# Loading a resident adjacency matrix with converting transfers in place of staged loads and casts

## The chip, the cores and the metric

The kernel runs on one core of one Trainium2 chip. The metric is the device time of a run in microseconds (us). The runs of one kernel in one round of measurements lie within 0.1 to 0.5% of each other.

Engine names in the profile: PE is TensorE (matmul), PEld its weight loads, DVE is VectorE, ACT is ScalarE, POOL is GpSimd, SP is SyncE. L214 is line 214 of the kernel that a view belongs to.

## The reference, cut to what matters

Four graph layers in sequence on x (8 x 2048 x 64), each followed by a residual sum and a layer norm. All four use the same adjacency matrix, 2048 x 2048 of zeros and ones.

```python
x = layernorm(x + hypergraph(x, H, adj, ...))        # layer 0: softmax over H, degrees and product with adj
x = layernorm(x + gcn(x, adj, W))                    # layer 1
x = layernorm(x + chebyshev(x, emb, adj, ...))       # layer 2
x = layernorm(x + causal(x, adj, v, W1, b1, W2, b2)) # layer 3: three steps of adj @ v, relu, linear

# in layer 0:
h   = x @ W
deg = maximum(adj.sum(-1), 1.0)
industry = einsum('nm,bmf->bnf', adj / deg[:, None], x @ W_ind)
```

The matrix, 16.8 MB, is kept in SBUF all along, as 16 tiles of 128x2048 in float32r, the type in which this kernel gives it to TensorE.

## The kernel before: the parts that matter

**Loading.** Each tile comes in four pieces of 256 KB over SP's queue into one of four staging buffers; GpSimd casts each piece into the resident tile. Nine tiles are asked for early, two when the features are done with, five later.

```python
def staged(name):
    return hy.tile([P, JT, P], F32, tag="x", name=name, bufs=4)

def load_adj(t):
    for c in range(NCH):                       # NCH = 4
        a = staged("a").rearrange("p t f -> p (t f)")
        nc.sync.dma_start(a, adj_t[t * P:(t + 1) * P, cols(c)])
        tc.keep_in_program_order(nc.gpsimd.tensor_copy(adj[t][:, cols(c)], a))
```

**Part A of layer 0.** A set-up (masks, iotas, ranks, small loads on GpSimd's queue), then a loop over 16 tiles of nodes. Its first instructions on VectorE stand behind a copy of a small loaded vector, `av_col`:

```python
for dst, v in ((fcb_col, fc_b), (av_col, av)):
    nc.gpsimd.dma_start(dst, v.rearrange("(n o) -> n o", o=1))
...
nc.gpsimd.memset(avz, 0.0)
nc.vector.tensor_copy(avz[:, b, s], av_col.to_broadcast([P, F]))
...
for t in range(NT):                            # NT = 16
    ...  # ph: 4 matmuls of xt[t]
    nc.vector.tensor_scalar(sv, hv[...], CLIP, -CLIP, op0=ALU.min, op1=ALU.max)   # "seen"
    ...  # exps on ACT, st and ex on DVE
    nc.scalar.dma_start(hs_hbm[t * P:(t + 1) * P, :], st)
    nc.tensor.matmul(pagg[...], lhsT=m_n[:, t, :], rhs=ex[...])                   # twice
```

**The slot stage of layer 0.** First the one-hot matrices and the scores. Then 57 slots: for each a product `pz`, nine filler matmuls (column sums of the adjacency for the degrees first, then the product with x), a multiply of `pz` on VectorE, an exponential on ScalarE and so on.

**The check in the last layer.** Each piece of the matrix is loaded once more and compared with the resident tile; differences are counted.

```python
def check():
    t, k = checks.pop(0)                       # 64 of them
    a = fcav.rearrange("p i b f -> p (i b f)")
    nc.sync.dma_start(a, adj_t[t * P:(t + 1) * P, cols(k)])
    nc.vector.scalar_tensor_tensor(
        a, a, 1.0, adj[t][:, cols(k)].bitcast(F32), op0=ALU.mult, op1=ALU.not_equal,
        accum_out=left[:, t, k:k + 1],
    )
```

## Time and profile before

| what | before |
|---|---|
| median of 4 runs | 2236.3 us (2230.7 to 2238.3) |
| span of the profiled run | 2233.4 us |
| part A ends (last `pagg` matmul) | 72.5 us |
| first slot multiply on VectorE | 93.7 us |
| first product of layer 2 with the adjacency | 952.3 us |
| first check | 1703.1 us |

The busy line of the page gives, for each engine, busy us, share of the span and instructions. The DMA-issue line gives the destination and source, the engine, the count, the KB of each and the median us from issue to landing.

```profile
PE 1989.5 (89%) x7330; PEld 1284.9 (58%) x7330; DVE 1136.6 (51%) x1875; ACT 337.4 (15%) x620; POOL 563.5 (25%) x539
```

```profile
a<-in_adj_t SPq DMA_DIRECT2D x64, 256.0 KB, 4.3
```

They show that TensorE is busy over most of the span and that GpSimd, whose casts the change removes, is busy for a quarter of it. So the change can only pay in a stage in which something waits for a cast or for a staged load.

### The profile page before, as it was taken

To read this page: it belongs to the slowest core of one execution; us is meant where nothing else is said; L and a number is where in the kernel's file an instruction comes from. 1 tells how busy PE (TensorE), PEld (TensorE's weight loads), DVE (VectorE), ACT (ScalarE), POOL (GpSimd) and SP (SyncE) were. 2 spreads that over 40 slices of the span, in tenths; PEclk is the share of its full clock that TensorE was granted. 3 is DMA by queue.
4 is the path that set the end of the run, shared out by engine and by line. 5 is a ranking of instruction groups with operands and counts; after the bars stand their busy time and mean duration, and the time that the engine had idled before them with its cause. 6 is when DMAs were issued, how large, how long until landed. Compare 5 with 4: busy or idle time off the path is not lost.

```text
span 2233.4 us, 19857 instructions
## 1 busy us (share of the span) xinstructions
PE 1989.5 (89%) x7330; PEld 1284.9 (58%) x7330; DVE 1136.6 (51%) x1875; ACT 337.4 (15%) x620; POOL 563.5 (25%) x539
## 2 busy tenths in 40 slices
PE   6789978988858999899999999999986989999994
PEld 4567744655644444375456456447433767787873
DVE  6559956666533223215864772782784344331312
ACT  1133333223111111010010001001000011111110
POOL 4666657564323323200010110110010001020202
PEclk9889989999979999999999999999997999999997
DMA  8622233222210000000000000000001223200000
GB/s 279 213 81 96 86 105 105 80 72 66 76 45 0 19 19 19 10 33 5 7 7 3 7 10 0 10 7 3 7 7 28 76 71 82 70 20 1 19 1 21
DMA packets 72619, 104.31 MB, mean 47 GB/s; under 512 B 28080, under 2 KB 28128, under 8 KB 72320
## 3 DMA queue, kind: packets, MB, share of 16 engines
q1 hardware_dynamic: 63648, 87.29, 12.5%
q0 software_dynamic: 3552, 9.10, 1.6%
q10 hardware_dynamic: 5312, 6.56, 0.9%
q8 instruction: 60, 0.98, 0.2%
q14 instruction: 47, 0.39, 0.1%
HBM read 76.11 MB, written 26.80 MB: 46 GB/s over the span
## 4 chain that ended last, share of the span: by engine, by line
PE 57%; DVE 15%; DMA 12%; POOL 8%; issue 5%; ACT 2%; SPq 1%; ACTq 0%; POOLq 0%; DVEq 0%
PE py L1009 18%; PE u L177 12%; PE u L956 10%; PE u L565 9%; DMA fcav<-in_adj_t 7%; POOL ln_r L156 3%; DMA a<-in_adj_t 2%; PE ug L177 2%; DVE fcav L1103 2%; POOL gn L751 1%; PE pr L177 1%; DVE ln_c L146 1%; DVE ln_v L152 1%; DVE ln_m L144 1%; PE pf L177 1%
## 5 line engine op out<-in xcount | busy, mean ns | idle before, releaser
L1009 PE MATMUL py<-wp,xg 128*128 128x512 f32 x1024 | 448.6, 597 | 8.4 <-DVE fcav L1014 5.8
L1009 PEld LDWEIGHTS py<-wp,xg 128*128 128x128 f32 x1024 | 193.8, 191 | 254.2 <-issue 216.0
L177 PE MATMUL u<-adj,hi 128*128 128x512 f32 x768 | 256.7, 416 | 0.0
L177 PE MATMUL u<-adj,lo 128*128 128x512 f32 x768 | 246.7, 400 | 0.9 <-DVE lo L1068 0.9
L956 PE MATMUL u<-pt,xn 128*128 128x512 f32 x512 | 230.6, 610 | 8.3 <-DVE u L965 7.1
L1014 DVE TENSOR_TENSOR fcav<-py,emb_n 128x512 f32<-128x512 f32 x256 | 177.1, 692 | 52.0 <-PE py L1009 37.1
L1017 POOL TENSOR_TENSOR r<-r,bias 128x256 f32<-128x256 f32 x32 | 23.3, 729 | 636.1 <-DVE r L1015 636.1
L1015 DVE TENSOR_REDUCE r<-fcav 128x32 f32<-128x512 f32 x256 | 175.4, 685 | 8.1
L956 PEld LDWEIGHTS u<-pt,xn 128*128 128x128 f32 x512 | 98.7, 195 | 131.8 <-issue 116.9
L565 PE MATMUL u<-adj,vh 128*128 128x512 f32 x512 | 159.0, 410 | 14.6 <-ACT vh L168 10.8
L177 PEld LDWEIGHTS u<-adj,hi 128*128 128x128 f32 x768 | 143.3, 190 | 40.8 <-issue 11.6
L177 PEld LDWEIGHTS u<-adj,lo 128*128 128x128 f32 x768 | 144.8, 190 | 35.0 <-DVE lo L1068 1.3
L565 PE MATMUL u<-adj,vl 128*128 128x512 f32 x512 | 152.5, 399 | 0.0
L156 POOL TENSOR_TENSOR ln_r<-ln_e,neg_half 128x8 f32<-128x8 f32 x64 | 106.7, 1666 | 171.8 <-DVE ln_e L154 171.2
L950 DVE TENSOR_SCALAR pt<-pt 128x512 f32<-128x512 f32 x64 | 48.8, 780 | 176.6 <-ACT pt L949 175.1
L1087 POOL TENSOR_TENSOR r<-r,xn 128x512 f32<-128x512 f32 x16 | 20.4, 1277 | 419.5 <-DVE r L1086 419.5
L565 PEld LDWEIGHTS u<-adj,vh 128*128 128x128 f32 x512 | 96.5, 190 | 44.8 <-ACT vh L168 12.3
L954 POOL TENSOR_TENSOR acc<-acc,pt 128x512 f32<-128x512 f32 x60 | 79.6, 1327 | 165.7 <-DVE pt L950 162.9
L565 PEld LDWEIGHTS u<-adj,vl 128*128 128x128 f32 x512 | 96.9, 190 | 22.2 <-issue 0.7
L1103 DVE SCALAR_TENSOR_TENSOR fcav<-fcav,adj 128x512 f32<-128x512 f32 x64 | 44.8, 699 | 119.3 <-DMA fcav<-in_adj_t 119.1
L150 ACT ACTIVATE r<-ln_c 128x512 f32<-128x512 f32 x64 | 40.4, 631 | 283.8 <-DVE ln_c L146 274.0
L751 POOL DMA_INDIRECT gn<-gs_hbm,rank x64 | 69.5, 1086 | 38.8 <-PE pg L180 15.8
(331 smaller groups left out, 2765.4 us busy)
## 6 DMA issues: line engine op xcount, KB each, us to landing
a<-in_adj_t SPq DMA_DIRECT2D x64, 256.0 KB, 4.3
fcav<-in_adj_t SPq DMA_DIRECT2D x64, 256.0 KB, 2.9
x_hbm<-r SPq DMA_DIRECT2D x20, 256.0 KB, 2.1
hs_hbm<-st ACTq DMA_DIRECT2D x16, 292.0 KB, 4.7
xt<-in_x_t SPq DMA_DIRECT2D x16, 256.0 KB, 5.0
xc<-in_x_n SPq DMA_DIRECT2D x16, 256.0 KB, 2.8
gs_hbm<-acc SPq DMA_DIRECT2D x16, 256.0 KB, 2.0
u_hbm<-ut SPq DMA_DIRECT2D x16, 256.0 KB, 2.5
```

Source lines behind the costliest of these rows:

```text
L150: nc.scalar.activation(r, xc, AF.Square)
L156: nc.gpsimd.tensor_tensor(rstd, vare, neg_half[:, :groups], ALU.pow)
L177: tc.keep_in_program_order(nc.tensor.matmul(*args, **kw))
L565: nc.tensor.matmul(u[c], lhsT=half[:, j, :], rhs=adj[t][:, cols(c)], start=t == 0 and i == 0, stop=ends and not own,)
L751: nc.gpsimd.indirect_dma_start(out=gn[:, j, :], out_offset=None, in_=g_rows, in_offset=bass.IndirectOffsetOnAxis(ap=rank4[:, p, c * JT + j ...
L950: nc.vector.tensor_scalar(pt, pt, 1.0, None, op0=ALU.max)
L954: nc.gpsimd.tensor_tensor(acc, acc, pt, ALU.add)
L956: nc.tensor.matmul(u[p], lhsT=xn[p][:, t, :], rhs=pt, start=t == 0, stop=t == NT - 1)
L1009: nc.tensor.matmul(py.rearrange("p o d -> p (o d)"), lhsT=xg[b][:, q, cols(j, P)], rhs=wp[:, q, cols(k)], start=q == 0, stop=q == 1,)
L1014: nc.vector.tensor_tensor(pr, py, e_b, ALU.mult)
L1015: nc.vector.tensor_reduce(r[:, j, b, cols(k, OH)], pr, AX.X, ALU.add)
L1103: nc.vector.scalar_tensor_tensor(a, a, 1.0, adj[t][:, cols(k)].bitcast(F32), op0=ALU.mult, op1=ALU.not_equal, accum_out=left[:, t, k:k + 1],)
```

## The change

Its intent: no staging buffers, no casts, one DMA instruction for each 1 MB tile. The loads go to GpSimd's queue, since only it issues transfers that convert (the Trainium skill, "DMA: Bandwidth & Descriptors", section "SWDGE vs HWDGE vs iDMA"). Room for 14 early tiles (before: 12) comes from holding x's tiles in a ring of eight. The loads are paced by copies of one column on GpSimd, `seen_x`, which wait for x's tiles. The check of the last layer now compares the reloaded piece with its own float32r copy.

```diff
     def load_adj(t):
-        for c in range(NCH):
-            a = staged("a").rearrange("p t f -> p (t f)")
-            nc.sync.dma_start(a, adj_t[t * P:(t + 1) * P, cols(c)])
-            tc.keep_in_program_order(nc.gpsimd.tensor_copy(adj[t][:, cols(c)], a))
+        tc.keep_in_program_order(nc.gpsimd.dma_start(adj[t], adj_t[t * P:(t + 1) * P, :]))
...
-    XT = NT // 4
-    EARLY = 9
+    XT = NT // 8
+    XB = XT * NP
...
-        xt = [xs.tile([P, NP, P], F32, name=f"xt{t}") for t in range(NT)]
-        for t in range(NT):
-            nc.sync.dma_start(xt[t], x_t[t])
+        # fetch_xt(t): tile of a ring of XB = 8; eight ahead, then one for each turn of part A
...
-        for t in range(EARLY):
+        for t in range(NT - XT):
+            ahead = min(t + 4, XB - 1)
+            tc.keep_in_program_order(nc.gpsimd.tensor_copy(seen_x, xt[ahead][:, 0, 0:1]))
             load_adj(t)
...
-        for t in range(EARLY, EARLY + 2):
+        for t in range(NT - XT, NT):
             load_adj(t)
...
-        for t in range(EARLY + 2, NT):
-            load_adj(t)
...
-                fill(4 if t == 0 and s < 6 else 9)
+                fill(9)
...
             nc.sync.dma_start(a, adj_t[t * P:(t + 1) * P, cols(k)])
+            ar = lp.tile([P, C], F32R, tag="r", name="ar", bufs=1)
+            nc.scalar.copy(ar, a)
             nc.vector.scalar_tensor_tensor(
-                a, a, 1.0, adj[t][:, cols(k)].bitcast(F32), op0=ALU.mult, op1=ALU.not_equal,
+                a, a, 1.0, ar.bitcast(F32), op0=ALU.mult, op1=ALU.not_equal,
```

More of the change, by code (lines that the diff above doesn't have):

```diff
@@ L270, in tile_gnn_fast @@
         xs = xs_scope.enter_context(tc.tile_pool(name="xs", bufs=1, side="right"))
+        seen_x = pa.tile([P, 1], F32, name="seen_x")
         m_n = pa.tile([P, NT, E], F32, name="m_n")
@@ L275, in tile_gnn_fast, with fetch_xt @@
             nc.scalar.dma_start(m_en[c], h_en[:, cols(c)])
-        xt = [xs.tile([P, NP, P], F32, name=f"xt{t}") for t in range(NT)]
-        for t in range(NT):
-            nc.sync.dma_start(xt[t], x_t[t])
+        xt = {}
+        def fetch_xt(t):
+            if t < NT:
+                xt[t] = xs.tile([P, NP, P], F32, tag="xt", name="xt", bufs=XB)
+                nc.sync.dma_start(xt[t], x_t[t])
+        for t in range(XB):
+            fetch_xt(t)
         bd66 = pa.tile([P, 2, F + 2], F32, name="bd66")
@@ L425, in tile_gnn_fast @@
                 )
+            fetch_xt(t + XB)
             hv = ph[:, :, 0:G * (F + 2)].rearrange("p k (g c) -> p k g c", c=F + 2)
```

## The prediction

> **What bounds the kernel now.** I read the page's busy shares first: PE is at 89%, so over most of the span TensorE sets the time. The change touches only the load phase and the adjacency checks near the end, so I cut the span into windows of 25 us, the first six shown. The columns are window, its length, then busy us of PE, PE weight loads, DVE, ACT and POOL with counts, granted clock, DMA share, GB/s.
>
> ```profile
> 0.00:25.00 25.00, 7.71 (x58) 6.49 (x58) 13.67 (x52) 2.88 (x10) 9.65 (x43) 0.96 0.88 261
> 25.00:50.00 25.00, 20.47 (x106) 13.17 (x106) 16.48 (x51) 4.07 (x21) 10.99 (x20) 0.90 0.89 297
> 50.00:75.00 25.00, 18.56 (x88) 11.87 (x89) 15.24 (x43) 3.97 (x19) 9.22 (x16) 0.93 0.81 272
> 75.00:100.00 25.00, 20.69 (x92) 15.55 (x91) 11.23 (x27) 5.24 (x14) 21.08 (x35) 0.82 0.53 165
> 100.00:125.00 25.00, 17.17 (x44) 10.82 (x43) 12.02 (x18) 7.72 (x12) 19.61 (x23) 0.70 0.70 213
> 125.00:150.00 25.00, 22.88 (x114) 18.73 (x113) 11.66 (x20) 6.27 (x12) 13.23 (x12) 0.86 0.02 7
> ```
>
> Three stages show. Up to 75 us ("part A": layer 0's projections, ranks, the hs rows stored to HBM) the DMA engines are the fullest resource. From 75 to 125 us the adjacency's second half comes in and POOL is fullest, because each 128x512 piece needs a POOL cast of 613 ns (64 of them, 39 us in all, from the view by tile). From 150 us on PE and DVE are both nearly full: this is the slot loop of layer 0, 57 slots with nine product matmuls between each.
>
> Next I read the timeline of the first 75 us, for part A's first and last dependent instructions:
>
> ```profile
> 3.53 0.59 POOL L401 DMA_DIRECT2D av_col<-in_av  x1
> 19.46 0.29 DVE L411 COPY fcav<-av_col 128x64 f32<-128x64 f32 x2
> 35.59 0.17 DVE L430 TENSOR_SCALAR seen<-ph 128x16 f32<-128x16 f32 x1 [0.53 <-PE ph L422]
> 68.19 0.16 DVE L430 TENSOR_SCALAR seen<-ph 128x16 f32<-128x16 f32 x1
> 70.60 1.87 PE L451 MATMUL pagg<-ex,m_n 128*64 128x260 f32 x4 [1.18 <-DVE ex L446]
> ```
>
> The reader is to see a small load issued at 3.5 us, its consumer on DVE at 19.46 us, and part A's end at 72.47 us (70.60 + 1.87). The fifth tile's clip is at 35.59 and the sixteenth's at 68.19: eleven tiles in 32.6 us. Where nothing disturbs it, two consecutive clips are 2.36 us apart (44.61 to 46.98), so eleven would take 26.0; the missing 6.6 us are waits of ACT and DVE on crowded stores.
>
> **What the Trainium skill says.** "DMA: Bandwidth & Descriptors", section "SWDGE vs HWDGE vs iDMA": a float32r destination always casts, and a cast can only be issued from GpSimd. So the 16 new loads share one queue with every other GpSimd load. The trace agrees that this queue is separate: its software_dynamic line has 3552 packets, against 63648 on SP's. The same page, "Queues, rings and completion order": descriptors are consumed in ring order on each DMA engine. No trace here shows it yet for a small load behind large ones; the changed kernel will. "Perfetto Trace Analysis", section "DMA Instruction — SWDGE (GPSIMD)": the profiler's end of such an issue is the end of descriptor generation, not the landing. The trace agrees (0.59 us for the issue above, 7.4 us to landing). No page I read gives the speed of a converting transfer.
>
> **The change part by part.**
>
> *Removed:* 64 casts (39 us of POOL) and 64 SP loads through four staging buffers. In the slot loop's start this mattered: the series of DVE slot multiplies, one for each slot, starts at 93.2 us and reaches the tenth slot at 136.1, 42.9 us for nine, while the other 48 (136.1 to 295.2) take 3.3 us each. Nine at 3.3 are 30, so 13 us can be won; another 1 because POOL starts the one-hots right behind a cast. Gain: **14 us**.
>
> *Moved, and this decides:* I built both programs and compared the static order on POOL. In the changed one, the first 14 loads stand **before** the mask, the iotas, the caps and the five kinds of small loads (av_col among them), which stood before all casts earlier. POOL executes in order. The program's waits show that the loads rotate over eight semaphores: the ninth adjacency load waits for the first to have landed, and so on. Hence the mask and iota that part A's first real matmul needs wait for the sixth tile; av_col's issue for the eighth; the memset of fcav that DVE's copy of av_col needs, for the twelfth; and av_col's data stands behind the fourteenth in the ring. On DVE that copy (19.46 us above) stands ahead of everything in part A's loop, also in the changed order. So the loop starts when the adjacency queue is empty.
>
> When is that? The loads start behind the x tiles (landed at some 11 to 14 us): say 13. They bring 14 x 1.05 = 14.7 MB, and 1.5 MB of xc and x go beside: 16.2 MB. Rate: the first 75 us moved 297 GB/s at a DMA share of 0.89, so 334 when full; and one load of 8 KB rows says the same:
>
> ```profile
> xn<-x_hbm ACTq DMA_DIRECT2D x1, 1024.0 KB, 4.7
> bp<-in_b_pool SPq DMA_DIRECT2D x1, 4.0 KB, 1.5
> ```
>
> 1.05 MB in 4.7 - 1.5 us is 328 GB/s. At 330 the queue is empty at 13 + 49 = 62, av_col there at 63. From that copy to the end part A took 72.5 - 19.5 = 53.0 us; with the DMA engines now free take off the 6.6: 46.4. Part A ends at 63 + 46 = 109 instead of 72.5: **37 us later**. Everything behind it (hs rows, aggregates, one-hots, slots) hangs on it.
>
> *Added at the end:* each of the 64 checks of the last layer gets an ACT copy between its load and its DVE compare, in a buffer shared with the output rows. One check in the timeline:
>
> ```profile
> 1783.48 0.69 DVE L1103 SCALAR_TENSOR_TENSOR fcav<-fcav,adj 128x512 f32<-128x512 f32 x1 [2.24 <-DMA fcav<-in_adj_t]
> 1787.08 0.69 DVE L1103 SCALAR_TENSOR_TENSOR fcav<-fcav,adj 128x512 f32<-128x512 f32 x1 [2.90 <-DMA fcav<-in_adj_t]
> ```
>
> A check repeats every 3.6 us and DVE stands for over 2 of them. The chain of waits names this load with 6.7% of the span, but that isn't its cost. The DVE ReLUs of pair 0 (37 checks) span 131.6 us from its first to the next pair's first, of pair 1 120.8, of pair 2 (no checks) 116.2: 64 checks cost some 20 us. With the copy (0.62 us as the hi casts) a check repeats every 4.5 us or so, but the new order spreads them, about 18 to each pair and up to five between two ReLUs: 5 x 4.5 = 22.5 against a pitch of 18.5. By that count some 7 us before the first ReLU and 4 to 9 for each pair, 26 instead of 20: **+6 us**, an estimate.
>
> Sum: 37 - 14 + 6 = +29 us: 2237.8 + 29 = **2267 us**.
>
> **The rivals.**
> 1. *The loads overlap part A as intended.* For it: the x pacing and the ring show that this was wanted, and DMA bytes alone would allow it. Against: the order on POOL and the wait of av_col. If the fourteen issues went out without holding POOL, part A would start near 30 us, share the DMA engines and end at some 80 to 87 (24.9 MB at 290 to 330 GB/s from about 2 us): +8 to +14 - 14 + 6, about 2240.
> 2. *Conversion is slow.* Nothing in this trace measures it. At 250 GB/s the queue needs 65 us instead of 49 (+16: 2283), at 165 GB/s twice 49 (+49: 2316).
> 3. *The late start is hidden.* If the slot loop had slack, the delay would shrink; but PE and DVE are both over 85% busy from 150 to 275 us, so it shifts whole.
> 4. *The checks become the bound of the last layer.* 64 x 4.5 = 288 us fits in its 530, so only the groups with five can be held; ACT waiting with DVE could make it 20 us worse.
>
> **Range and chances.** Rival 1 gives the low end, 2240; rival 2 at half speed or rival 4 on top gives 2308. I take 62% for within 2% (under 2282.6), 36% for slower, since a converting rate under some 250 GB/s is enough, and 2% for faster: that needs 45 us, and the load phase can't give more than 14 even without any delay.
>
> **What would show it.** Right: POOL's mask and iota only after about 30 us; DVE's copy of av_col near 63 us with a wait on POOL or on a load; a loop pitch near 2.4 us after it; part A's last aggregate matmul near 109 us; the tenth slot about 30 us after the first; DVE compares of the last layer 4 us or more apart. Wrong: an av_col copy before 45 us (the queue isn't the gate), an adjacency tile taking over 5 us each (conversion slow), or the last layer's span changed by over 15 us.

## The result, and the profile after

The changed kernel took 2262.0 us (median of 4 runs, 2258.7 to 2264.8), the kernel before 2236.3. The ratio is 1.0118, with a 95% interval of 1.0093 to 1.0144. A ratio here is the mean time of one kernel's runs over the mean of the other's of the same rounds, so not quite the ratio of the two medians. The change is 1.2% slower, inside the predicted range.

Where the time went, by the same marks in both traces:

| stretch | before, us | after, us | difference |
|---|---|---|---|
| start to VectorE's copy of `av_col` | 19.5 | 57.4 | +37.9 |
| from there to the end of part A | 53.0 | 41.4 | -11.6 |
| to the first slot | 21.2 | 20.3 | -0.9 |
| first slot to layer 2's first product with the adjacency | 858.6 | 846.8 | -11.8 |
| from there to the first check | 750.9 | 751.0 | +0.2 |
| first check to the end | 530.3 | 540.1 | +9.8 |
| span | 2233.4 | 2256.9 | +23.5 |

The windows of 25 us after the change, with the columns of the prediction's (window, length, busy us of PE, PEld, DVE, ACT, POOL, granted clock, DMA share, GB/s):

```profile
25.00:50.00 25.00, 6.78 (x50) 6.18 (x50) 4.06 (x15) 0.24 (x1) 7.33 (x35) 0.93 1.08 420
50.00:75.00 25.00, 13.34 (x67) 8.47 (x68) 13.95 (x55) 3.34 (x19) 1.66 (x4) 0.66 0.46 155
75.00:100.00 25.00, 23.96 (x133) 15.91 (x131) 19.56 (x58) 4.90 (x29) 0.00 (x0) 1.00 0.47 173
```

From 25 to 50 us the DMA engines move 420 GB/s, nearly all of it adjacency, and the compute engines stand almost still: VectorE works for 4 us where it worked for 16.5 before. Then part A runs with the DMA engines half idle. The two kinds of work take turns instead of overlapping.

The timeline of the changed kernel (start, length, engine, line, operation, out<-in, and in brackets the idle time before it and what released it) shows why:

```profile
11.89 0.76 POOL L214 DMA_DIRECT2D adj<-in_adj_t  x1
...
24.03 0.53 POOL L214 DMA_DIRECT2D adj<-in_adj_t  x1 [1.49 <-DMA adj<-in_adj_t]
...
35.18 0.53 POOL L214 DMA_DIRECT2D adj<-in_adj_t  x1 [1.77 <-DMA adj<-in_adj_t]
35.72 0.30 POOL masks.py:66 TENSOR_SCALAR_AFFINE_SELECT tri<-tri 128x128 bf16<-128x128 bf16 x1
...
40.17 0.56 POOL L407 DMA_DIRECT2D av_col<-in_av  x1 [1.66 <-DMA adj<-in_adj_t]
...
52.38 0.33 POOL L414 MEMSET fcav<- 128x256 f32 x1
...
57.40 0.30 DVE L417 COPY fcav<-av_col 128x64 f32<-128x64 f32 x2 [15.88 <-DMA av_col<-in_av]
...
95.66 0.17 DVE L437 TENSOR_SCALAR seen<-ph 128x16 f32<-128x16 f32 x1 [0.32 <-PE ph L428]
...
97.68 1.09 PE L458 MATMUL pagg<-ex,m_n 128*64 128x260 f32 x4 [1.04 <-DVE ex L453]
```

The first adjacency load goes out at 11.9 us and the ninth at 24.0, after waiting for a tile to land. The mask of the set-up comes only behind the fourteenth load, at 35.7. The small load of `av_col` goes out at 40.2 (3.5 before), its data are copied at 57.4 (19.5 before), and the last of sixteen clips is at 95.7, the end of the last aggregate at 98.8. The trace's DMA packets put the end of the fourteenth tile at 56.4: the small load was in only a microsecond after the large ones in front of it, as the prediction expected of one queue.

In the last layer, the waits between the first check and the end. Columns: engine, what waited, at which line, for whom: us in total, times, longest. First before, then after:

```profile
DVE fcav L1103 <- DMA fcav<-in_adj_t: 119.1, 55, 3.2
```

```profile
DVE fcav L1109 <- ACT ar L1108: 174.3, 63, 4.8
ACT ar L1108 <- DMA fcav<-in_adj_t: 143.7, 51, 4.2
ACT ar L1108 <- DMA out_x<-r: 64.4, 12, 7.5
```

The compare now waits for the copy on ScalarE, and the copy waits for its load or, twelve times, until the output rows have left the buffer `r` that it shares: up to 7.5 us for one.

### The profile page after: what moved, and what is told of

It reads as the page before. It is cut to its first block, busy times and chain, and to the rows that moved or that the text cites. A ratio compares the mean times of both kernels' runs of the same rounds, so it can differ in the third digit from the quotient of the medians.

```text
span 2256.9 us, 19846 instructions
## 1 busy us (share of the span) xinstructions
PE 1981.6 (88%) x7330; PEld 1279.6 (57%) x7330; DVE 1138.0 (50%) x1875; ACT 373.6 (17%) x684; POOL 538.3 (24%) x505
## 3 DMA queue, kind: packets, MB, share of 16 engines
q1 hardware_dynamic: 54432, 70.51, 10.4%
## 5 line engine op out<-in xcount | busy, mean ns | idle before, releaser
L1109 DVE SCALAR_TENSOR_TENSOR fcav<-fcav,ar 128x512 f32<-128x512 f32 x64 | 44.3, 692 | 174.5 <-ACT ar L1108 174.3
L1091 POOL TENSOR_TENSOR r<-r,xn 128x512 f32<-128x512 f32 x16 | 20.5, 1280 | 431.4 <-DVE r L1090 431.4
```

Source lines behind the costliest of these rows:

```text
L1109: nc.vector.scalar_tensor_tensor(a, a, 1.0, ar.bitcast(F32), op0=ALU.mult, op1=ALU.not_equal, accum_out=left[:, t, k:k + 1],)
```

## The experiments

Twelve kernels ran; all gave correct results. The ratio to the kernel before is that of the same rounds. The marks are those of the table above: copy of `av_col`, end of part A, first slot, the stretch from the first slot to layer 2's first product with the adjacency ("slots": the 57 slots take about 200 us of it, the rest is layer 1 and the softmax part of layer 2), and the stretch from the first check to the end ("last").

| run | median us | ratio, 95% interval | av_col | part A ends | first slot | slots | last |
|---|---|---|---|---|---|---|---|
| before | 2236.3 | 1 | 19.5 | 72.5 | 93.7 | 858.6 | 530.3 |
| changed | 2262.0 | 1.0118 (1.0093-1.0144) | 57.4 | 98.8 | 119.0 | 846.8 | 540.1 |
| e1_old_check | 2251.4 | 1.0064 (1.0051-1.0078) | 56.3 | 97.8 | 118.1 | 850.3 | 531.3 |
| e2_new_check_only | 2247.2 | 1.0046 (1.0033-1.0059) | 19.0 | 71.6 | 94.6 | 860.3 | 539.5 |
| e3_setup_first | 2252.6 | 1.0076 (1.0062-1.0091) | 19.4 | 81.1 | 110.4 | 847.4 | 539.9 |
| e4_small_on_act | 2249.9 | 1.0063 (1.0048-1.0077) | 38.0 | 90.2 | 110.5 | 846.2 | 539.0 |
| e7_setup_ones_first | 2245.6 | 1.0040 (1.0020-1.0061) | 19.5 | 81.1 | 101.6 | 849.3 | 542.3 |
| e10_ones_first_old_check | 2236.4 | 1.0002 (0.9986-1.0019) | 19.0 | 81.9 | 102.5 | 847.4 | 531.3 |
| e8_fill4 | 2260.2 | 1.0103 (1.0081-1.0124) | 58.4 | 99.6 | 119.9 | 846.7 | 542.1 |
| e9_nine_early | 2224.4 | 0.9948 (0.9930-0.9966) | 19.6 | 74.1 | 94.2 | 846.4 | 531.2 |
| e11_five_late | 2232.3 | 0.9970 (0.9950-0.9989) | 19.5 | 73.0 | 92.8 | 856.5 | 531.4 |
| e14_dummy_casts | 2242.8 | 1.0031 (1.0014-1.0047) | 19.2 | 72.0 | 97.3 | 857.4 | 531.3 |
| e9b_seven_early | 2227.2 | 0.9962 (0.9945-0.9978) | 19.6 | 71.3 | 95.1 | 845.7 | 531.8 |
| e16_lows_on_dve | 2225.3 | 0.9935 (0.9922-0.9949) | 19.9 | 73.9 | 94.7 | 845.4 | 532.7 |

The theory to test: the loss is the late set-up (part A held until the adjacency queue is empty) plus the new check, less a gain in the slots. Rivals: the loss lies in a slow conversion or in crowded DMA engines, and the parts do not add up.

### The check alone, both ways

e1_old_check is the changed kernel with the old compare:

```diff
-            ar = lp.tile([P, C], F32R, tag="r", name="ar", bufs=1)
-            nc.scalar.copy(ar, a)
             nc.vector.scalar_tensor_tensor(
-                a, a, 1.0, ar.bitcast(F32), op0=ALU.mult, op1=ALU.not_equal,
+                a, a, 1.0, adj[t][:, cols(k)].bitcast(F32), op0=ALU.mult, op1=ALU.not_equal,
```

> The changed kernel with the check of the kernel before (compare with the resident tile, no ACT copy). My theory: the last layer from the first check to the end falls from 540.8 us to about 530, the load phase stays as in the changed kernel, and the time falls by 8 to 12 us to about 2251. Rival (the last layer is longer for another reason, the clock say): no difference beyond 3 us.

e2_new_check_only is the same edit in the other direction, on the kernel before.

> The kernel before with the new check alone (ACT copy in the buffer shared with the output rows). My theory: 8 to 12 us more than before, 2244 to 2248 us, all in the last layer; a check every 4.3 us instead of 3.6, spread over all four pairs. Rival (copy hidden, ACT is only a sixth busy): within 3 us of before.

The last layer took 531.3 us with the old check in the changed kernel and 539.5 with the new check in the kernel before. So the new check costs about 9 us in the traces (8.8 and 9.2), and 10.7 and 11.0 us by the medians, in either kernel. The waits of e2 are those of the changed kernel:

```profile
DVE fcav L1105 <- ACT ar L1104: 172.8, 63, 4.2
ACT ar L1104 <- DMA fcav<-in_adj_t: 142.6, 51, 4.2
```

e1 also found no difference between reloaded and resident values (a difference would have sent the kernel to its slow general path): for these zeros and ones the conversion by the transfer is exact, so the old check is usable with it.

### The set-up ahead of the loads

e3_setup_first moves the fourteen loads with their pacing behind the set-up's GpSimd work. e4_small_on_act leaves them and issues the set-up's seven small loads from ScalarE.

```diff
-        for t in range(NT - XT):      # ahead of the set-up
-            ahead = min(t + 4, XB - 1)
-            tc.keep_in_program_order(nc.gpsimd.tensor_copy(seen_x, xt[ahead][:, 0, 0:1]))
-            load_adj(t)
...
         nc.gpsimd.dma_start(age, bass.AP(tensor=a_ge.tensor, ...))   # the last small load
+        for t in range(NT - XT):
+            ahead = min(t + 4, XB - 1)
+            tc.keep_in_program_order(nc.gpsimd.tensor_copy(seen_x, xt[ahead][:, 0, 0:1]))
+            load_adj(t)
```

> The changed kernel, with the fourteen early loads moved behind POOL's setup work (mask, iotas, caps, memsets and the seven small loads) and nothing else altered. My theory (POOL's order and the queue behind it hold part A back): DVE's copy of av_col falls from 57 us back to about 20 us, part A ends between 73 and 87 us instead of 99, and the whole takes 2236 to 2250 us, so 12 to 26 us less than the changed kernel. Rival (the sheer bytes of fourteen early tiles hold part A back, whatever the order): the copy moves forward, but part A's loop crawls on stores and x tiles and still ends at 95 us or later, and the time stays within 5 us of 2262.

```diff
-            nc.gpsimd.dma_start(dst, v.rearrange("(n o) -> n o", o=1))
+            nc.scalar.dma_start(dst, v.rearrange("(n o) -> n o", o=1))
...           # the same for fc_w and w_ind (twice each) and age
```

> The changed kernel, with the seven small loads (av_col and the like) issued from ACT's queue instead of GpSimd's; the adjacency loads still stand ahead of the mask and the iotas on POOL. It parts the delay into its two steps. My theory: the mask still comes at about 35.7 us (it waits for the sixth tile), but av_col no longer waits for tiles eight to fourteen, so part A's loop starts at about 41 to 42 us instead of 57.4, shares the DMA engines with the last tiles until about 57, and ends at 83 to 88 instead of 99: 2246 to 2252 us. If instead the wait for av_col were only apparent (DVE held by something else), the loop would still start near 57 us and the time would stay at 2262.

Both confirm the gate: the copy of `av_col` comes at 19.4 and 38.0 us instead of 57.4. Part A ends 17.7 and 8.6 us earlier, less than half of what the start gained; e4 expected 83 to 88 us and came to 90.2. The reason that e3's trace gives is that part A now shares the DMA engines with the adjacency. A wait between 20 and 82 us:

```profile
ACT st L440 <- DMA hs_hbm<-st: 33.7, 9, 10.4
```

ScalarE waits nine times, up to 10.4 us, for a buffer whose small rows have not left for HBM, while the DMA engines move 411 GB/s from 25 to 50 us, most of it adjacency. From the third tile on, the loop's pitch (from one clip to the next) is 3.7 to 4.6 us, once 7.4, until the fourteen tiles are in; then it is 2.1. The section "Fewer loads early" tests this reading.

e3 missed its expected time by 2.6 us. Its first slot came 29 us after part A, not 20. The timeline of e3 shows a new wait:

```profile
82.46 1.40 POOL L237 DMA_INDIRECT hrow<-hs_hbm,order  x1 [42.01 <-DVE agg L505]
84.15 1.30 POOL L237 DMA_INDIRECT hrow<-hs_hbm,order  x1 [0.30 <-issue]
85.45 1.18 POOL L214 DMA_DIRECT2D adj<-in_adj_t  x2
86.57 0.76 POOL L478 CAST ones_r<-ones 128x128 fp32r<-128x128 f32 x1
...
87.39 8.45 PE L177 MATMUL du<-adj,ones_r 128*128 128x512 f32 x24 [6.33 <-POOL ones_r L478]
```

The tile of ones, the weights of all degree matmuls, is copied by GpSimd. In e3 this copy had fallen behind the gathers and the last two adjacency loads, and GpSimd works in order. e7_setup_ones_first also puts this copy ahead of the loads:

```diff
+        ones_r = hy.tile([P, P], F32R, name="ones_r")
+        tc.keep_in_program_order(nc.gpsimd.tensor_copy(ones_r, ones))
+
         for t in range(NT - XT):      # the loads, as in e3
...
-        ones_r = hy.tile([P, P], F32R, name="ones_r")
-        nc.gpsimd.tensor_copy(ones_r, ones)
```

> The run with the setup ahead of the loads (e3) took 2252.6 us, and its slot stage began 29 us after the end of part A, not 20, with TensorE waiting for the tile of ones that GpSimd copied only behind the last two adjacency loads. This run also puts that copy ahead of the loads. If that wait was on the path: the first slot about 20 us after part A instead of 29, and about 2243 us in all. Rival: the slot stage's start is held by the late loads or by the degree products instead; then the first slot stays near 29 us after part A and the time stays at 2252.

The first slot came 20.5 us after part A, and the time fell by 7 us to 2245.6 (expected: about 2243). The same stretch of e7 on TensorE, from the end of part A:

```profile
80.68 0.38 PE L460 MATMUL pagg<-ex,m_n 128*64 128x260 f32 x1
80.99 5.89 PE L177 MATMUL du<-adj,ones_r 128*128 128x512 f32 x24
```

The degree matmuls now follow the last aggregate at once. e10_ones_first_old_check is e7 with the old check.

```diff
-            ar = lp.tile([P, C], F32R, tag="r", name="ar", bufs=1)     # on top of e7
-            nc.scalar.copy(ar, a)
...
+                a, a, 1.0, adj[t][:, cols(k)].bitcast(F32), op0=ALU.mult, op1=ALU.not_equal,
```

> Setup and the tile of ones ahead of the loads, and the old check (compare of the adjacency tile with itself, no copy on ScalarE). If the last layer's 10 us and the late setup's 17 us and the ones' 9 us add up: 2231 to 2238 us, equal to the kernel before within 0.3%. Rival: the parts overlap, and some of them comes back as another wait; then 2240 or more.

It took 2236.4 us, equal to the kernel before. The three repairs add up: by the medians 9.4 us for the set-up (e3), 7.0 for the ones (e7) and 9.2 for the check, together 25.6 of the 25.7 that were lost. They don't bring back the kernel before, though: part A still ends 9.4 us later than there, and the gain in the slots pays for it.

### Fewer loads early

What part A still loses in e10 (81.9 against 72.5 us) should be the share of the DMA engines that fourteen early tiles take. e9_nine_early asks for nine early, as the kernel before did, and for seven when part A is done.

```diff
-        for t in range(NT - XT):      # on top of e10
+        for t in range(9):
...
         fetch_rows(1)
-        for t in range(NT - XT, NT):
+        for t in range(9, NT):
             load_adj(t)
```

> As the run with ones first and old check, but with nine tiles of adjacency loaded early, as before, and seven after the features' rows were fetched. If the rest of the lost time in part A is the loads' share of the DMA engines: part A ends near 72 to 75 us, the first slot near 93, the slot stage keeps its 12 us, and the time is 2220 to 2228 us, under both kernels. Rival: the degree products, which need all sixteen tiles, then wait for the late loads (7 MB at some 400 GB/s is 17 us): the first slot near 105 us and the time 2234 or more.

It took 2224.4 us, 0.5% under the kernel before. Part A ends at 74.1 us and the slots keep their 12 us; the seven late tiles are issued from 78.5 us on and land until 99, five of them before the first slot at 94.2 (344 GB/s from 75 to 100 us), and the degree matmuls hardly wait (0.2 us).

e9b_seven_early is e9 with seven early and nine late (9 becomes 7 in both loops).

> As the nine-early run, with seven tiles early and nine late. Two fewer megabytes compete with part A's stores: at the loop's disturbed pitch of 4 us against 2.1, some 2 tiles of the loop gain 2 us each, so part A ends near 70 us and the time is about 2220. Rival: nine late tiles (9.4 MB at some 400 GB/s, 24 us) now hold the degree products, whose results the first slot needs within 20 us; then the first slot is no earlier than 94 us and the time stays at 2224 or rises.

Part A ends 2.8 us earlier than in e9, but the first slot is 0.9 us later: the degree matmuls now wait 4.6 us for the late tiles, as the rival said. It took 2227.2 us, a ratio that cannot be told from e9's. Nine is enough.

### Where the slots' 12 us come from

e8_fill4 is the changed kernel with the filler of before in the first six slots.

```diff
-                fill(9)
+                fill(4 if t == 0 and s < 6 else 9)
```

> The changed kernel with the short filler of before (four products in each of the first six slots, not nine). The stretch from the first slot to layer 2 took 846.8 us in the changed kernel and 858.6 in the one before. If the full filler is what gave the 12 us: this stretch about 856 us and the time 2266 to 2273 us. Rival: the slots became faster because GpSimd no longer casts and no late tile lands between them; then the stretch stays within 3 us of 847 and the time at 2262.

The slots took 846.7 us, as with the full filler (kernels whose slot stage is the same differ by some 5 us in the table, from 845.4 to 850.3): it was not the filler. Two parts of the old loading remain, the casts on GpSimd and the late landing of the last tiles; each was put back alone into e9. e14_dummy_casts adds 28 copies on GpSimd that nobody reads:

```diff
         for t in range(9, NT):        # after fetch_rows, on top of e9
             load_adj(t)
+        for t in range(9, 11):
+            for c in range(NCH):
+                tc.keep_in_program_order(nc.gpsimd.tensor_copy(
+                    hy.tile([P, C], F32, tag="x", name="a", bufs=4), adj[t][:, cols(c)].bitcast(F32)))
...
+        # and the same for t in range(11, NT), where the kernel before cast its last five tiles
```

> The nine-early run (2224.4 us; 846.3 us from the first slot to layer 2, where the kernel before took 858.6) with 28 GpSimd copies of 128x512 added: after their load, tiles 9 to 15 are copied to a buffer that nobody reads, in the places where the kernel before had its casts. If the casts on GpSimd were what slowed the first slots: this stretch 854 us or more, most of the 12 us back, and about 2232 to 2236 us. Rival: the casts fitted into GpSimd's gaps and the late arrival of the tiles was the cost; then within 3 us of 846 and 2224 us.

e11_five_late issues the last five loads where the kernel before did, without casts:

```diff
-        for t in range(9, NT):
+        for t in range(9, 11):
             load_adj(t)
...
+        for t in range(11, NT):       # at the end of the slots' set-up
+            load_adj(t)
```

> The nine-early run, but tiles 11 to 15 are issued where the kernel before issued them, at the end of the set-up of the slots, still as converting loads without casts. If the late arrival of these tiles was the cost: the stretch from the first slot to layer 2 at 854 us or more and 2232 to 2236 us. If the casts were: within 3 us of 846, and 2222 to 2228 us.

Both put most of it back: the slots take 857.4 us with the casts and 856.5 with the late tiles. I had posed them as rivals, and they are not: each costs time by itself. In e14, GpSimd is held for 12 us in one piece, and the one-hots of the next slots, with the matmuls that need them, stand behind it (first its timeline, then a wait of TensorE from 70 to 165 us):

```profile
94.52 12.14 POOL L560 COPY a<-adj 128x512 f32<-128x512 f32 x20
```

```profile
PEld ps L177 <- POOL o L254: 19.6, 17, 11.5
```

In e11 TensorE waits for the tiles themselves. The waits of the kernel before from 93 to 165 us show the degree products waiting for casts, which themselves wait for loads (first fence); those of e11 from 70 to 165 us show them waiting for the loads (second fence):

```profile
PEld du L177 <- POOL adj L217: 7.9, 9, 1.6
```

```profile
PEld du L177 <- DMA adj<-in_adj_t: 4.2, 2, 2.3
```

e14 is not a true copy of the old casts. It holds GpSimd in one block, and its first slot is 5 us later than e9's in relation to part A; this took it above its expected time. In e11, one of six runs took 2221.8 us and the others 2230.0 to 2233.3. A narrower mark is surer, because equal kernels agree within 2 us up to the last slot and differ by 5 only behind it. From the first to the 57th slot multiply it is 201.6 us before, 191.4 after the change and 191.6 in e9; with the casts (e14) 202.0, with the late tiles (e11) 197.8. So of the 12 us some 10 lie in the slots themselves; casts in one block put back all of these, late tiles about 6. How the gain divides between the two in the kernel before stays open; what is shown is that taking away only one of them is not enough.

### A hold on VectorE that looked like the next cost

The changed kernel and e9 both have a strange interval: the second slot comes 9.7 and 9.4 us after the first. In e9's timeline the 128x8 maximum on VectorE lasts 5.36 us, and it ends with the fourth of four GpSimd subtractions. VectorE first, then GpSimd:

```profile
92.89 0.25 DVE L675 TENSOR_SCALAR rs<-rs 128x8 f32<-128x8 f32 x1
...
96.90 5.36 DVE L675 TENSOR_SCALAR rs<-rs 128x8 f32<-128x8 f32 x1
102.18 0.68 DVE L703 SCALAR_TENSOR_TENSOR y<-pz,y 128x512 f32<-128x512 f32 x1
```

```profile
97.19 1.30 POOL L169 TENSOR_TENSOR v0l<-xc,v0h 128x512 fp32r<-128x512 f32 x1
98.44 1.29 POOL L169 TENSOR_TENSOR v1l<-xc,v1h 128x512 fp32r<-128x512 f32 x1
99.67 1.30 POOL L169 TENSOR_TENSOR v2l<-xc,v2h 128x512 fp32r<-128x512 f32 x1
100.93 1.30 POOL L169 TENSOR_TENSOR v3l<-xc,v3h 128x512 fp32r<-128x512 f32 x1
```

The Trainium skill, "SBUF — State Buffer", section "SBUF: two separate sides", says that GpSimd shares one pair of ports with VectorE, that for VectorE operations which use this pair it is an exclusive lock and not a split of bandwidth, and that the loser is blocked entirely. The trace agrees: the same operation takes 0.25 us at 92.89 and 5.36 us beside the subtractions. e16_lows_on_dve moves the four subtractions to VectorE, into a gap ahead of the first slot:

```diff
             for c in range(NCH):
-                parts(0, c)           # split with the subtraction on GpSimd
+                part[c] = split(pb, xc.pop((0, c)), f"v{c}", 1, [P, JT, P])
```

> The nine-early run with one change: the four 128x512 subtractions that split the first features (v0l to v3l) go from GpSimd to VectorE. In the nine-early run VectorE's 128x8 maximum lasts 5.36 us, from 96.90 to 102.26, and ends with GpSimd's four subtractions (97.19 to 102.23); the same operation takes 0.25 us at 92.89. VectorE is idle for 3.3 us before, from 88.6 to 91.9, where four subtractions of 0.68 us fit. If the two engines' shared path holds VectorE: the maximum takes under 0.5 us, the second slot comes some 5 us after the first instead of 9.4, the tenth about 35 us after it instead of 39.6, and the time falls by 3 to 5 us, ratio to the kernel before 0.9925 to 0.994 against 0.9948. Rival: the slots are paced by TensorE's own products there; then the maximum is short, but the tenth slot stays near 39 us and the time at 0.995.

The maximum shrank to 0.28 us:

```profile
97.41 0.28 DVE L675 TENSOR_SCALAR rs<-rs 128x8 f32<-128x8 f32 x1
```

The second slot then came 6.4 us after the first instead of 9.4, but the tenth 38.3 after it instead of 39.6, and layer 2's first product with the adjacency began at 940.1 us instead of 940.5. The time is 2225.3 us, its ratio 0.9935 against 0.9948 with overlapping intervals. The rival fits: the slots of this stretch are paced by TensorE, as the window of e16 indicates (24.36 busy of 25 us):

```profile
100.00:125.00 25.00, 24.36 (x112) 19.96 (x111) 12.55 (x21) 5.90 (x9) 9.35 (x6) 0.86 0.09 33
```

So the hold is real, and taking it away gains nothing here that the noise lets one see.

### What was not tried

A load into the resident tile as plain float32, without conversion, was refused when compiled, so it has no run. The ring of eight x tiles and the pacing copies were not varied by themselves.

## Why the prediction was right, point by point

It said 2267 us (2240 to 2308), most likely within 2%; 2262.0 came, 5 us less. That the miss is so small is partly luck: the first term was 11 us too large, the third 4 too small and the second hid two errors, and they cancel in part. Its three terms, and what the traces gave:

| term | predicted | measured |
|---|---|---|
| end of part A later | +37 | +26.3 |
| slots, and the way to them | -14 | -12.8 |
| new check | +6 | +9.8 |
| sum | +29 | +23.5 in the spans, with 0.2 us elsewhere (25.7 by the medians) |

- **The gate.** Right, and the step that decided the direction. The mask came at 35.7 us ("only after about 30 us"), and `av_col`'s copy waited 15.9 us for its load. e3 and e4 removed two parts of the gate and the copy moved to 19.4 and 38.0 us.
- **When the queue is empty.** The step "at 330 the queue is empty" was mis-sized: the copy came at 57.4 us, not 63. With the converting transfers the DMA engines moved 420 GB/s from 25 to 50 us. I had taken the rate from a mixed stage (297 GB/s at a share of 0.89, which is the window from 25 to 50 us and not the first 75) and from one 1 MB load. The Trainium skill, "DMA: Bandwidth & Descriptors", section "Bandwidth", has 341 GB/s for 1 MB and 425 for 16 MB issued from GpSimd; the second, for much data at once, was the one to use; the 420 measured here is close to it.
- **Part A behind the gate.** Predicted 46 us, measured 41.4. One step that failed is "Where nothing disturbs it, two consecutive clips are 2.36 us apart": that pair was not yet undisturbed. With half-idle DMA engines the clips from 74.5 to 95.7 us are 2.12 us apart (ten intervals), and the eleven intervals took 23.3 us, not 26.0. This is 2.7 of the 5 us. The rest lies where the prediction corrected nothing: from the copy to the fifth clip 15.0 us (16.1 before), from the last clip to the end 3.1 (4.3 before). Together with the rate this is the whole difference in the first term: 5.6 and 5 us.
- **The slots.** The gain was right in size, by luck: its working was wrong. The multiply at 136.1 us that I called the tenth is the ninth, and the first starts at 93.7, not 93.2; the tenth starts at 140.3, so the nine intervals took 46.6 us. And they did not shrink to "about 30 us" but to 39.7: the step that failed is "Nine at 3.3 are 30". TensorE was busy for 24.36 of 25 us in such a stretch (e16), so that its own work there, and not the 3.3 us of a later slot, looks like the limit. So 6.9 us came from the first nine intervals where 13 were forecast, 3.3 from the later slots and 1.7 behind the last one, where I had expected none; the 1.7 are within what equal kernels differ by.
- **The check.** The direction was right (a compare every 4.35 us in the median, 3.63 before), the term too small: 9.8 us, not 6. The copy's wait for the output rows in the shared buffer (64.4 us over twelve waits) was named and not counted. That it makes up the other 4 us is argued only; no run gave the copy its own buffer.
- **The rivals.** "Conversion is slow" is refuted (420 GB/s; from 33 to 45 us a tile landed about every 2.5 us). "The loads overlap part A as intended" is what e3 built on purpose, and its part A ended at 81.1 us, inside the 80 to 87 that I had given. "Hidden" is refuted: when the repairs brought the first slot forward by 8.6 us (e3) and 8.8 (e7), the whole time fell by 9.4 and 7.0. "The checks become the bound" did not come: the last layer grew by 9.8 us, and this rival had named 20.

## What to carry to other kernels

Before moving a stream of large loads to an engine's queue, look at what else that engine issues and in what order: here the saving from the old staged loads and casts was real (12 us), and the place of fourteen issues ahead of a handful of small loads and masks took it back twice over (26 us). Put the small set-up first, then only as many large loads as the next stage can share the DMA engines with, and the rest where those engines are idle: with the set-up and the tile of ones in front, nine early tiles and the old check, the converting loads win 0.5% (2224.4 us). When an instruction looks held for a long time, first look whether the engine that paces the stage is idle in that window.

## What the Trainium skill lacked or had wrong

- "DMA: Bandwidth & Descriptors", section "Bandwidth": no rate for a transfer that casts. While the changed kernel's 128x2048 loads from float32 to float32r streamed, the DMA engines moved 420 GB/s (from 25 to 50 us, a little other traffic included), close to the 425 that the page gives for 16 MB.
- The same page, section "Queues, rings and completion order": it says that an engine takes turns between rings packet by packet, but gives no figure for what small stores lose beside large loads. Here, in traffic of 411 GB/s that was mostly loads with 8 KB rows, ScalarE waited nine times for stores of 292 KB, 33.7 us in all and up to 10.4.
- "SBUF — State Buffer", section "SBUF: two separate sides": it describes the lock for one instruction of each engine, not for several in a row. In this trace a 128x8 operation of VectorE stayed blocked over four consecutive GpSimd instructions, 5.36 us, against 0.28 without them; it did not get in between two of them.
